# Context laid out as three chunks of 64 dims, projected in 64-row tiles, with a copy between keys and values

## The chip, the cores and the metric

The program runs on one core of one Trainium2 chip. A core has several engines that run side by side, each through its own instruction queue and strictly in that queue's order: TensorE (PE) for matmuls, VectorE (DVE), ScalarE (ACT), GpSimd (POOL), and SyncE (SP), which here only issues DMAs. Matmuls write to PSUM, which here is handed out in tiles; VectorE and ScalarE read results from there. The metric is the device time of one execution in microseconds, as the median of several runs.

## What is computed

A perceiver of four layers. `x` (128 tokens of 256) attends to a long context (12,544 tokens of 192), then to itself, then passes a feed-forward of experts. The part that matters here is the attention over the context in layers 0 to 2; layer 1 stands for the three (layer 0 has a mask in place of biases and clip, layer 2 no clip):

```python
def _L1_xattn_ref(query, key_value, Wq, bq, Wk, bk, Wv, bv, Wo, bo):
    H, D = 16, Cq // 16
    q = (query @ Wq + bq).reshape(B, Nq, H, D).transpose(0, 2, 1, 3)
    k = (key_value @ Wk + bk).reshape(B, Nkv, H, D).transpose(0, 2, 1, 3)
    v = (key_value @ Wv + bv).reshape(B, Nkv, H, D).transpose(0, 2, 1, 3)
    attn = jnp.clip(jnp.einsum('bhqd,bhkd->bhqk', q, k) * D ** -0.5, -CLAMP, CLAMP)
    attn = jax.nn.softmax(attn, axis=-1)
    attn = jnp.where(jnp.any(jnp.isnan(attn)), 1.0 / Nkv, attn)
    return jnp.einsum('bhqk,bhkd->bqhd', attn, v).reshape(B, Nq, Cq) @ Wo + bo
```

`key_value` is the context. It must be multiplied by Wk and Wv (192 x 256 each), which is the work that the change rearranges. Layer 3 does the same with 1,024 columns.

## The kernel before

All is in float32 but for a few small tiles. The context comes from memory with its dims on the partitions, in 25 blocks of 512 tokens (the last has 256). A block has two halves of 256 tokens. Its 192 dims do not fit 128 partitions, so it is held as two tiles: `ctxA` (dims 0 to 127, all 512 tokens, 256 KB) and `ctxB` (dims 128 to 191; half 0 on partitions 0 to 63, half 1 on 64 to 127; 128 KB). `Net.context` (L383) issues both loads, one block ahead of the one asked for, into four buffers each. Wk and Wv lie alike: the first 128 rows in one slab, the last 64 rows twice, once for each half of the partitions (`load_kv`).

`Keys` projects for layers 0 to 2. The 16 heads are taken in two groups `g` of 8, so `cols` picks 128 of the 256 columns. `project(g, b, low)` is called with `low` 0 and then 1. With `low` 0 it takes a PSUM tile `pair` (128 x 2 x 512, one 512-column part for each half of the block), and multiplies `ctxA` into keys (columns 0 to 255 of each part) and values (columns 256 to 511): two key products of 256 columns and four value products of 128 columns, over 128 rows. With `low` 1 it adds the `ctxB` products to the same places: two and four products over 64 rows, those of half 0 on the upper rows of the array and those of half 1 on the lower. Then ScalarE copies the keys out (`keep_keys`, L131, or L133 with bias) and after them the values (`keep_values`, L137). Every program matmul of float32 shows in the trace as two records.

`attend_twice` goes over the blocks twice for each group. In the first pass it finds the highest score of each query; its loop runs 25 steps. A step projects a block that later steps need (`keys.project`, both values of `low` in one go), and then makes score products in 32-row tiles:

- Layer 0 (`masked`): `highest` twice, each with two `pair` tiles of products (a mask row, L558, and the keys, L559), and VectorE reduces each pair to maxima (L565).
- Layers 1 and 2: `over` makes products with the difference of two blocks' keys (`apart`, made on POOL, L570) into two pairs, and ScalarE applies Relu to each (L578); then `highest_of_two` makes products with a block's keys into two more pairs, which VectorE adds and reduces (L586).

There are four `pair` tiles in the first pass (`psum(ppr=4)`), used in turn; a step that projects uses five. `in_order` fixes the order on TensorE, VectorE and ScalarE inside a step as the code has it. In group 0 of layers 1 and 2 the first 8 blocks are projected earlier, during the layer before, in a `kv` tile of which there is one (`early`, `early_pair`); in layer 0 the first two. Of the remaining blocks the last three are projected with keys only, their values by `project_values` near the end of the pass. The second pass makes weights and adds up values; at its end in group 0, blocks 0 and 1 of group 1 are projected.

In layer 1 POOL also adds up the whole context in group 0 (`add_up`), for a guard against NaN (`nan_guard`), which multiplies the sums by Wk and Wv.

Layer 3 uses `KeysInTurn`, a subclass of `Keys` with the same `keys_into` and `values_into` over `ctxA` and `ctxB`, two blocks at a time, with loads two blocks ahead.

The lines by which the profile names this work: L103 is every projection matmul (tiles `pair`, `kv` or `v`), L131 and L133 the key copies, L137 the value copies, L395 and L397 the loads of `ctxA` and `ctxB`.

Of the kernel before, what the change touches and what calls it, by code (L numbers as in the profile page):

```python
# [12 lines left out]
F32 = mybir.dt.float32  # L13
# [4 lines left out]
ALU = mybir.AluOpType  # L18
AX = mybir.AxisListType
PSUM = bass.MemoryType.PSUM  # L20

P = 128
D = 256
CD = 192
CB = CD - P
H = 16
S2 = 12544
SB = 512
HB = SB // 2
# [24 lines left out]
class Keys:  # L54
# [4 lines left out]
    def __init__(self, net, wk, wv, groups, bias=None, sums=None):  # L59
        self.net, self.nc, self.wk, self.wv, self.bias, self.sums = net, net.nc, wk, wv, bias, sums  # L60
        self.context = net.context(groups * NSB)
        self.started, self.done, self.rest = {}, 0, None
        if sums is not None:
            self.nc.gpsimd.memset(sums, 0.0)
# [30 lines left out]
    def add_up(self, g, b):  # L95
        if g == 0 and self.sums is not None:
            a, c = self.context(b)
            n = HB * len(self.halves(b))
            self.nc.gpsimd.tensor_tensor(self.sums[:, :n], self.sums[:, :n], a[:, :n], ALU.add)
            self.nc.gpsimd.tensor_tensor(self.sums[:, SB:], self.sums[:, SB:], c, ALU.add)  # L100

    def mm(self, out, a, b, low, start):
        self.nc.tensor.matmul(out, a, b, start=start and not low, stop=low == 1, skip_group_check=True)  # L103

    def keys_into(self, p, g, low, blocks, turn=None):

        cols = slice(g * P, g * P + P)
        for j, b in enumerate(blocks):  # L110
            ctx = self.context((g if turn is None else turn) * NSB + b)[low]
            for i, r in self.halves(b):
                r = r if low else slice(0, P)
                keys = ctx[r, :HB] if low else ctx[:, i * HB : (i + 1) * HB]
                self.mm(p[:, i, j * HB : (j + 1) * HB], self.wk[r, low, cols], keys, low, j == 0)

    def values_into(self, p, g, low, blocks, first=0, turn=None):
        cols = slice(g * P, g * P + P)
        for j, b in enumerate(blocks):
            ctx = self.context((g if turn is None else turn) * NSB + b)[low]  # L120
            for c in range(2):
                for i, r in self.halves(b):
                    at = first + (2 * j + c) * P
                    r = r if low else slice(0, P)
                    k = c * P if low else i * HB + c * P
                    self.mm(p[:, i, at : at + P], ctx[r, k : k + P], self.wv[r, low, cols], low, first + j + c == 0)
# [26 lines left out]
    def project(self, g, b, low, values=True):  # L153


        if g * NSB + b < self.done:
            return
        if not low:
            self.add_up(g, b)
            self.started[g, b] = self.net.early_pair() if self.rest is None else self.net.pair()  # L160
        p = self.started[g, b]
        self.keys_into(p, g, low, [b])
        if values:
            self.values_into(p, g, low, [b], HB)
        if low:
            n = len(self.halves(b))
            self.keep_keys(g, b, p[:, :n, :HB])
            if values:
                self.keep_values(g, b, p[:, :n, HB:])
            self.done = g * NSB + b + 1  # L170

    def project_values(self, g, blocks):
        p = self.net.pair()
        for low in range(2):
            self.values_into(p, g, low, blocks)
        for j, b in enumerate(blocks):
            self.keep_values(g, b, p[:, : len(self.halves(b)), j * HB : (j + 1) * HB])


class KeysInTurn(Keys):  # L180
# [5 lines left out]
    def __init__(self, net, wk, wv):  # L186
        self.net, self.nc, self.wk, self.wv = net, net.nc, wk, wv
        self.context = net.context((GROUPS3 + 1) * NSB, 2)
        self.first = {}

# [16 lines left out]
class Net:  # L207
# [123 lines left out]

    def load_column(self, src, pool, name):

        t = pool.tile([P, 2], F32, tag=name, name=name, bufs=1)
        self.nc.sync.dma_start(t, src.rearrange("o (g p) -> p (o g)", p=P))
        return t
# [46 lines left out]
    def context(self, until, ahead=1):  # L383

        nc, d = self.nc, self.d
        made = []

        def get(k):  # L390
            while len(made) <= k + ahead and len(made) < until:
                b = len(made) % NSB
                n = min(SB, S2 - b * SB)
                a = self.ahead.tile([P, SB], F32, tag="ctxA", name="ctxA", bufs=4)
                self.queue.dma_start(a[:, :n], d["ctxA"][:, b * SB : b * SB + n])  # L395
                c = self.ahead.tile([P, HB], F32, tag="ctxB", name="ctxB", bufs=4)
                self.queue.dma_start(c, d["ctxB"][b])  # L397
                made.append((a, c))
            return made[k]

        return get
# [617 lines left out]
    def l0_xattn(self, x):  # L1019
        nc, d = self.nc, self.d  # L1020
        with self.tc.tile_pool(name="x0", bufs=2, reuse_waits="tile") as pool:
            wk = self.load_kv(d["L0_xattn_Wk"], D, "wk", self.lw, nc.scalar)
            keys = Keys(self, wk, None, 2)
            keys.context(0)
            keys.wv = self.load_kv(d["L0_xattn_Wv"], D, "wv", self.lw, nc.scalar)
# [14 lines left out]
    def keys_biased(self, name, guarded):  # L1040

        nc, d = self.nc, self.d
        wk = self.load_kv(d[f"{name}_Wk"], D, "wk", self.lw)
        wv = self.load_kv(d[f"{name}_Wv"], D, "wv", self.lw)
        bk = self.load_column(d[f"{name}_bk"], self.lw, "bk")
        sums = self.lw.tile([P, SB + HB], F32, tag="sums", name="sums", bufs=1) if guarded else None
        keys = Keys(self, wk, wv, 2, bk, sums)

        self.queue = nc.gpsimd
        keys.early()  # L1050
        return keys
# [33 lines left out]
    def nan_guard(self, pool, totals, xT, wq, bq, wk, wv, bk, bv):  # L1085
# [4 lines left out]
        wide = pool.tile([P, 2, P], F32, tag="wide", name="wide")  # L1090
# [5 lines left out]
        def sums():  # L1096
            s = self.stat(2)
            nc.vector.tensor_reduce(s[:, 0:1], totals[:, :SB], AX.X, ALU.add)
            nc.vector.tensor_reduce(s[:, 1:2], totals[:, SB:], AX.X, ALU.add)
            nc.vector.tensor_copy(wide, bc(s, 2, P))  # L1100
            nc.gpsimd.memset(many, float(S2))

        def products(bank_pair):
            p = bank_pair()
            self.mm(p[:, 0, :D], [(xT[:, k, :], wq[:, k, :]) for k in range(2)] + [(self.ones[:1, :], bq)])
            self.mm(p[:, 1, :D], [(wide[:, k, :], wk[:, k, :]) for k in range(2)] + [(many, bk)])
            made.append(p)
            p = bank_pair()
            self.mm(p[:, 0, :D], [(wide[:, k, :], wv[:, k, :]) for k in range(2)])
            made.append(p)  # L1110
# [748 lines left out]
def layout(inputs):  # L1859
# [4 lines left out]
    ctx[:, :S2] = a["ctx_768"][0].T  # L1864
    given["ctxA"] = ctx[:P, :S2]
# [31 lines left out]
def program(given):  # L1897
    nc = bacc.Bacc("TRN2", target_bir_lowering=False, num_devices=1)
# [12 lines left out]
```

## Time and profile before

| | us |
|---|---|
| median of 3 runs | 3023.78 (3019.76 to 3024.86) |
| the profiled execution | 3021.48, of which the span of its instructions is 3019.8 |
| TensorE busy | 2882.8 (95%), mean granted clock 0.975 |
| VectorE, ScalarE, POOL busy | 2024.2, 1626.2, 282.7 |
| first pass with projections, layer 0 | 17.6 to 148 and 275.6 to 402, 5.62 a step in its regular part |
| first pass, layer 1 | 658 to 759 and 905.8 to 1027, 5.42 a step that projects |
| first pass, layer 2 | 1311 to 1413 and 1554 to 1674, 5.42 a step that projects |
| layer 3, keys and attention | from 1952 to about 2872, 9.35 for two blocks |

The stages are told by the starts of L103's key products on TensorE: a step is the time from one block's first key product to the next one's. "Busy" counts overlapping records once; records of matmuls overlap, since one starts before the one before it has ended. In a list of waits an engine is named with the line that waited, and after the arrow the engine and line whose work ended that wait.

### The profile page before, as it was taken

What the parts mean: (1) busy time and instruction counts of PE and PEld (TensorE: products, weight loads), DVE (VectorE), ACT (ScalarE), POOL (GpSimd) and SP (SyncE); (2) the same over time, 40 slices, a digit from 0 to 9 for tenths busy, and PEclk for the clock granted to TensorE, in tenths of its full rate; (3) what the DMA queues carried; (4) which work ended last, traced back from release to release, by engine and by line L of the source; (5) the groups of instructions that cost most, each with busy time, mean ns of one, the idle gap of its engine ahead of it and who ended that gap; (6) DMA issues with size and microseconds to landing.
All of it is one profiled execution on the core that took longest, in us unless ns stands there. A gap on an engine that the chain in (4) does not pass through costs nothing.

```text
span 3019.8 us, 79794 instructions
## 1 busy us (share of the span) xinstructions
PE 2882.8 (95%) x34893; PEld 2209.0 (73%) x34893; DVE 2024.2 (67%) x3241; ACT 1626.2 (54%) x1904; POOL 282.7 (9%) x504
## 2 busy tenths in 40 slices
PE   8999999989999999999999998899999999999969
PEld 5677667455676576765776675688989989889858
DVE  6876887525893598745544555577777777777844
ACT  1176148335685585245875682355655656555521
POOL 7011021223001100211001002000000000000000
PEclk9999999999999999999999998999999999999979
DMA  5201210562002202521012007232322223222436
GB/s 133 61 19 32 72 39 6 189 225 57 21 3 79 59 4 88 175 82 53 15 39 73 23 3 258 92 98 80 85 84 83 85 79 88 85 78 83 136 111 201
DMA packets 177706, 247.28 MB, mean 82 GB/s; under 512 B 32459, under 2 KB 119269, under 8 KB 177358
## 3 DMA queue, kind: packets, MB, share of 16 engines
q1 hardware_dynamic: 165592, 227.26, 24.8%
q0 software_dynamic: 11008, 14.37, 1.6%
q8 instruction: 274, 4.49, 0.6%
q10 hardware_dynamic: 758, 0.55, 0.1%
q14 instruction: 74, 0.61, 0.1%
HBM read 241.56 MB, written 0.13 MB: 80 GB/s over the span
## 4 chain that ended last, share of the span: by engine, by line
PE 83%; DVE 11%; ACT 2%; DMA 1%; issue 1%; SPq 1%; POOL 0%; ACTq 0%; DVEq 0%; POOLq 0%
PE pair L103 21%; PE acc L699 10%; PE pair L559 8%; PE v L103 8%; PE sc L859 6%; PE pair L629 5%; PE acc L901 5%; PE ps L279 5%; PE one L629 4%; DVE parts L565 3%; PE pair L622 2%; PE acc L279 2%; PE kv L103 2%; PE ps L1698 1%; DVE over L586 1%
## 5 line engine op out<-in xcount | busy, mean ns | idle before, releaser
L586 DVE CUSTOM_DVE_ANT_0 over<-over,pair 128x512 f32<-128x512 f32 x384 | 241.2, 683 | 249.2 <-PE pair L559 237.6
L103 PE MATMUL pair<-ctxA,wk 128*128 128x256 f32 x1236 | 328.7, 399 | 6.5 <-ACT over L578 1.8
L103 PEld LDWEIGHTS pair<-ctxA,wk 128*128 128x128 f32 x1236 | 217.0, 190 | 138.5 <-ACT over L578 53.0
L861 ACT COPY kept<-sc 128x1024 f32<-128x1024 f32 (+1 forms) x135 | 136.2, 1009 | 261.2 <-PE sc L859 261.2
L565 DVE TENSOR_REDUCE parts<-pair 128x2 f32<-128x1024 f32 (+1 forms) x216 | 235.7, 1157 | 41.8 <-PE pair L559 41.8
L290 DVE TENSOR_TENSOR top<-top,kept 128x1024 f32<-128x1024 f32 (+2 forms) x145 | 169.1, 1169 | 134.0 <-ACT kept L861 132.7
L293 DVE SCALAR_TENSOR_TENSOR e<-pair,floor 128x1024 f32<-128x1024 f32 x196 | 227.3, 1217 | 14.6 <-PE pair L629 14.6
L677 ACT ACTIVATE e<-pair 128x1024 f32<-128x1024 f32 x196 | 200.7, 1025 | 46.5 <-PE pair L629 26.0
L654 ACT ACTIVATE e<-e 128x1024 f32<-128x1024 f32 x196 | 206.7, 1057 | 35.3 <-DVE e L293 24.3
L629 PE MATMUL pair<-qz,kT 32*128 32x256 f32 x2112 | 218.9, 374 | 0.0
L699 PE MATMUL acc<-e,v 128*17 128x128 f32 x6336 | 211.4, 274 | 3.0 <-ACT e L692 2.2
L699 PEld LDWEIGHTS acc<-e,v 128*17 128x17 f32 x6336 | 155.8, 97 | 67.8 <-ACT e L692 45.6
L692 ACT ACTIVATE e<-e 128x1024 f32<-128x1024 f32 x196 | 205.0, 1048 | 0.0
L293 DVE SCALAR_TENSOR_TENSOR e<-one,maskcol,less 128x256 f32<-128x256 f32 x392 | 162.6, 477 | 53.3 <-PE one L629 43.3
L859 PE MATMUL sc<-qz,kT 64*128 64x128 f32 x2816 | 197.8, 279 | 0.0
L559 PE MATMUL pair<-kT,qz 32*128 32x512 f32 (+1 forms) x1120 | 192.7, 592 | 5.2 <-DVE parts L586 3.8
L578 ACT ACTIVATE over<-pair 128x1024 f32<-128x1024 f32 x192 | 186.9, 1021 | 14.7 <-PE pair L559 7.4
L103 PEld LDWEIGHTS v<-wv,ctxA 128*128 128x128 f32 x1568 | 189.8, 192 | 6.4 <-issue 1.7
L103 PE MATMUL v<-wv,ctxA 128*128 128x128 f32 x1568 | 193.1, 276 | 0.0
L103 PE MATMUL pair<-ctxB,wk 64*128 64x256 f32 x1236 | 188.9, 399 | 0.0
L290 DVE TENSOR_TENSOR e<-one,less 128x512 f32<-128x512 f32 x196 | 126.3, 686 | 88.6 <-PE pair L629 88.1
L859 PEld LDWEIGHTS sc<-qz,kT 64*128 64x128 f32 x2816 | 171.6, 187 | 13.0 <-issue 1.3
(457 smaller groups left out, 5637.7 us busy)
## 6 DMA issues: line engine op xcount, KB each, us to landing
ctxA<-in_ctxA SPq DMA_DIRECT2D x324, 256.0 KB
ctxB<-in_ctxB SPq DMA_DIRECT2D x339, 128.0 KB
w<-in_L_ffn_W SPq DMA_DIRECT2D x32, 1024.0 KB
ctxA<-in_ctxA POOLq DMA_DIRECT2D x36, 256.0 KB, 3.2
w<-in_L_ffn_w_gateT SPq DMA_DIRECT2D x8, 1024.0 KB
wu<-in_L_ffn_w_upT SPq DMA_DIRECT2D x8, 1024.0 KB
w<-in_L_ffn_w_downT SPq DMA_DIRECT2D x8, 1024.0 KB
w<-in_L_ffn_w1T SPq DMA_DIRECT2D x8, 1024.0 KB
```

Of the source, the lines that this page charges most:

```text
L103: self.nc.tensor.matmul(out, a, b, start=start and not low, stop=low == 1, skip_group_check=True)
L279: self.nc.tensor.matmul(out, lhsT, rhs, start=(i == 0), stop=(i == n - 1))
L290: self.nc.vector.tensor_tensor(out, a, b, op)
L293: self.nc.vector.scalar_tensor_tensor(out, a, s, b, op0, op1, **kw)
L559: nc.tensor.matmul(x, qz[r, g, s, :], k[r, :n], start=not by_mask, stop=True)
L565: nc.vector.tensor_reduce(parts[:, s, 2 * half : 2 * half + 2, i], x, AX.X, ALU.max)
L586: nc.vector.tensor_tensor_reduce(es[half][:, j, :], es[half][:, j, :], x[:, j, :], 1.0, -LARGEST, ALU.add, ALU.max, parts[:, s, 2 * half + ...
L629: nc.tensor.matmul(at, keys.kT(c // 4)[tiles[t], k], q, start=start, stop=True, skip_group_check=True)
L654: nc.scalar.activation(to, to, AF.Exp)
L692: nc.scalar.activation(to, to, AF.Exp)
L699: nc.tensor.matmul(acc[32 * t : 32 * t + 17, half, :], v[:, c % 4 + j, 4 * half + t, :], es[half][:, t // 2, j, t % 2, :], start=c + j + h ...
L859: nc.tensor.matmul(x[:, t, c : c + P], kT[r, c : c + P], qz[r, g, :], start=True, stop=True)
```

## The change

In layers 0 to 2 a block of context is one tile of 128 partitions x 3 x 256. Half 0 of the tokens lies on partitions 0 to 63, half 1 on 64 to 127; the middle index is the chunk of 64 dims. The host lays the input `ctx` out in this way, and one DMA of 384 KB loads it. Wk and Wv are held as three chunks of 64 rows, twice on the partitions (`load_twice`). Every projection product is over 64 rows: per block 6 for the keys and 12 for the values, in place of 4 and 8. `project` now has the keys in its first part, followed by their copy, and the values in its second, followed by theirs. `project_values`, `add_up` and the guard follow the new layout. Layer 3 keeps its layout and functions (moved into `KeysInTurn`); its A and B parts are now two regions of one tile, still loaded by two DMAs. The program also asks for a scratch of 8192 bytes for dynamic DMAs.

```diff
+CH = CD // CB
-        self.context = net.context(groups * NSB)
+        self.context = net.context(groups * NSB, whole=True)
...
-            a, c = self.context(b)
-            n = HB * len(self.halves(b))
-            self.nc.gpsimd.tensor_tensor(self.sums[:, :n], self.sums[:, :n], a[:, :n], ALU.add)
-            self.nc.gpsimd.tensor_tensor(self.sums[:, SB:], self.sums[:, SB:], c, ALU.add)
+            self.nc.gpsimd.tensor_tensor(self.sums, self.sums, self.context(b), ALU.add)
...
+    def keys_into(self, p, g, b):
         cols = slice(g * P, g * P + P)
+        ctx = self.context(g * NSB + b)
+        for c in range(CH):
             for i, r in self.halves(b):
+                self.mm(p[:, i, :HB], self.wk[r, c, cols], ctx[r, c, :], c == 0, c == CH - 1)
+
+    def values_into(self, p, g, b, first=0):
+        cols = slice(g * P, g * P + P)
+        ctx = self.context(g * NSB + b)
+        for half in range(2):
+            at = first + half * P
+            for c in range(CH):
+                for i, r in self.halves(b):
+                    self.mm(p[:, i, at : at + P], ctx[r, c, half * P : half * P + P], self.wv[r, c, cols], at + c == 0, c == CH - 1)
...
-    def project(self, g, b, low, values=True):
+    def project(self, g, b, part, values=True):
         if g * NSB + b < self.done:
             return
-        if not low:
+        n = len(self.halves(b))
+        if part == 0:
             self.add_up(g, b)
-            self.started[g, b] = self.net.early_pair() if self.rest is None else self.net.pair()
-        p = self.started[g, b]
-        self.keys_into(p, g, low, [b])
+            p = self.started[g, b] = self.net.early_pair() if self.rest is None else self.net.pair()
+            self.keys_into(p, g, b)
+            self.keep_keys(g, b, p[:, :n, :HB])
+            return
         if values:
-            self.values_into(p, g, low, [b], HB)
-        if low:
-            n = len(self.halves(b))
-            self.keep_keys(g, b, p[:, :n, :HB])
-            if values:
-                self.keep_values(g, b, p[:, :n, HB:])
-            self.done = g * NSB + b + 1
+            p = self.started[g, b]
+            self.values_into(p, g, b, HB)
+            self.keep_values(g, b, p[:, :n, HB:])
+        self.done = g * NSB + b + 1
...
+    def load_twice(self, src, n, name, pool, queue=None):
+        v = pool.tile([P, CH, n], F32, tag=name, name=name, bufs=1)
+        for i in range(2):
+            (queue or self.nc.sync).dma_start(v[i * CB : (i + 1) * CB], src.rearrange("(c p) n -> p c n", p=CB))
+        return v
...
-                n = min(SB, S2 - b * SB)
-                a = self.ahead.tile([P, SB], F32, tag="ctxA", name="ctxA", bufs=4)
-                self.queue.dma_start(a[:, :n], d["ctxA"][:, b * SB : b * SB + n])
-                c = self.ahead.tile([P, HB], F32, tag="ctxB", name="ctxB", bufs=4)
-                self.queue.dma_start(c, d["ctxB"][b])
-                made.append((a, c))
+                t = self.ahead.tile([P, SB + HB], F32, tag="ctx", name="ctx", bufs=4)
+                if whole:
+                    self.queue.dma_start(t, d["ctx"][b])
+                    made.append(t.rearrange("p (c k) -> p c k", c=CH))
+                    continue
+                n = min(SB, S2 - b * SB)
+                self.queue.dma_start(t[:, :n], d["ctxA"][:, b * SB : b * SB + n])
+                self.queue.dma_start(t[:, SB:], d["ctxB"][b])
+                made.append((t[:, :SB], t[:, SB:]))
...
-            self.mm(p[:, 1, :D], [(wide[:, k, :], wk[:, k, :]) for k in range(2)] + [(many, bk)])
+            self.mm(p[:, 1, :D], [(wide[:, k, :], wk[:, k, :]) for k in range(CH)] + [(many, bk)])
...
+    given["ctx"] = ctx.reshape(CH, CB, NSB, 2, HB).transpose(2, 3, 1, 0, 4).reshape(NSB, P, CH * HB)
...
-    nc = bacc.Bacc("TRN2", target_bir_lowering=False, num_devices=1)
+    nc = bacc.Bacc("TRN2", target_bir_lowering=False, num_devices=1, dynamic_dma_scratch_size=8192)
```

## The prediction

> **What bounds the kernel now.** I read the page's chain first:
>
> ```profile
> PE 83%; DVE 11%; ACT 2%; DMA 1%; issue 1%; SPq 1%; POOL 0%; ACTq 0%; DVEq 0%; POOLq 0%
> PE pair L103 21%; PE acc L699 10%; PE pair L559 8%; PE v L103 8%; PE sc L859 6%; PE pair L629 5%; PE acc L901 5%; PE ps L279 5%; PE one L629 4%; DVE parts L565 3%; PE pair L622 2%; PE acc L279 2%; PE kv L103 2%; PE ps L1698 1%; DVE over L586 1%
> ```
>
> TensorE carries 83% of it, and the projections of L103 are the largest item (layer 3's, which are also on L103, included). So the stage to read is the first pass of `attend_twice`, where each step projects one block. In layers 1 and 2 a step takes 5.42 us. TensorE's timeline of one step, then ScalarE's:
>
> ```profile
> 991.65 1.13 PE L103 MATMUL pair<-ctxA,wk 128*128 128x256 f32 x4
> 992.62 1.05 PE L103 MATMUL pair<-wv,ctxA 128*128 128x128 f32 x8
> 993.60 0.70 PE L103 MATMUL pair<-ctxB,wk 64*128 64x256 f32 x4
> 994.14 0.61 PE L103 MATMUL pair<-wv,ctxB 64*128 64x128 f32 x8
> 994.68 1.14 PE L559 MATMUL pair<-apart,qz 32*128 32x512 f32 x8
> 995.64 1.50 PE L559 MATMUL pair<-kT,qz 32*128 32x512 f32 x8
> ```
> ```profile
> 990.48 1.94 ACT L578 ACTIVATE over<-pair 128x1024 f32<-128x1024 f32 x2
> 994.80 0.69 ACT L133 ACTIVATE kT<-pair,bk 128x512 f32<-128x512 f32 x1 [2.38 <-PE pair L103]
> 995.38 0.58 ACT L137 COPY v<-pair 128x512 f32<-128x512 f32 x1
> 995.90 1.94 ACT L578 ACTIVATE over<-pair 128x1024 f32<-128x1024 f32 x2
> ```
>
> Columns: start, length, engine, line, what. Five `pair` tiles are needed per step and four exist, so a projection waits until the step before has freed its first one. The cycle closes through this:
>
> ```profile
> DVE over L586 <- PE pair L559: 46.4, 16, 2.9
> ...
> PEld pair L103 <- ACT over L578: 12.1, 16, 0.8
> ```
>
> These are the waits of 16 such steps (total, times, longest): the projection waits 0.76 us for the first L578. The ring is: projection 3.03 (991.65 to 994.68), difference products to the start of L578 1.22 (995.90), L578 1.02, its signal to TensorE 0.15; sum 5.42. VectorE idles 2.9 us a step, so it sets nothing.
>
> Layer 0 has another ring, of 5.62 us, through VectorE:
>
> ```profile
> 92.69 4.62 DVE L565 TENSOR_REDUCE parts<-pair 128x2 f32<-128x1024 f32 x4 [1.00 <-PE pair L559]
> ...
> 93.97 1.13 PE L103 MATMUL pair<-ctxA,wk 128*128 128x256 f32 x4
> ...
> 97.00 0.41 PE L558 MATMUL pair<-row,ones 32*128 32x512 bf16 x4
> ...
> 97.12 0.59 ACT L131 COPY kT<-pair 128x512 f32<-128x512 f32 x1 [4.54 <-PE pair L103]
> ```
>
> Projection 3.03, products to the first reduction 1.31 (97.00 to 98.31), reduction and signal 1.28. VectorE idles 1.00 us per step although it holds four reductions, so the projection's length is in this ring too. In both rings every us added to a projection is added to the step.
>
> **The change, part by part: one projection.** A program matmul shows as two records. Let p be the time of two paired 64-row records of 256 columns, v of 128 columns, l the first weight load that nothing hides, d the drain at a change of tile shape. From the starts above: L103's four B key records 2p+l=0.54, four A key records 4p+l=0.97, eight B value records 4v+d=0.54, eight A value records 8v+d=0.98. So p=0.215, l=0.11, v=0.11, d=0.10. The B rows show that two 64-row products in different row halves run side by side: eight records in the time of four.
>
> After: keys are three chunks for two halves, 6p+l=1.40; values 12v+d=1.42. Back to back that is 2.82 us against 3.03: the pairs cost what the old mixture cost, and one change of shape (128 to 64 rows) with its load is gone, −0.21. The Trainium skill, "TensorEngine Tiling (Array Packing)", section "Key Properties", says that changing the tiling mode drains TensorE. That agrees with d+l=0.21 here and would by itself give the −0.21.
>
> But the two parts are no longer back to back. In the changed program, as built, the first value product of a block waits for ScalarE's copy of that block's keys, in all 132 blocks with values (44 in each layer): the keys and the values of a half lie in one PSUM bank. Before, both copies followed all products. The wait lies in TensorE's queue: the value products stand behind it, then the step's score products, and ScalarE's L578 or VectorE's reduction behind these.
>
> Its price: the last key pair starts at l+5p=1.185, one such record lasts 0.376 (source view of L103), so keys end at 1.56. ScalarE starts 0.05 after the last record (994.75 to 994.80). The copy takes 0.69 with bias, 0.59 without. The signal back takes 0.15 (L578 ends 991.50, TensorE starts 991.65). ScalarE is free then: its second L578 ends 0.77 after the projection starts. Values start at 2.45 (layer 0: 2.35); they pay l again, so 12v+d+l=1.53, and the score products start at 3.98 (3.88) in place of 3.03. That is +0.95 (+0.85). In layers 1 and 2 L578 no longer queues behind the value copy (995.38 to 995.90 just covers its input's arrival), −0.05: +0.90.
>
> The skill's "PSUM — Partial Sum Buffer", section "Terms", has a rule that speaks against this change: two engines on one bank and quadrant at once are a collision error, so the copy and the value products of one bank must take turns. By that rule the price is +0.9 a step; without it, it would be −0.2. No run here shows such an error.
>
> Counts: layer 0 has 40 such steps in the loops; the first four last 7 to 11 us for loads, and I take half there: 36×0.85+4×0.43=32.3. Layers 1 and 2 have 14+20 each: 68×0.90=61.2.
>
> **The other parts.**
> - The end of the second pass in group 0, three times: two blocks are projected there. The first value wait also stands behind exponentials (until 905.29 in layer 1, projection from 902.73); other products of the order fill in for the second block. About 1.2 each by that timeline, bounds 0 and 2.6: +3.6.
> - The 18 blocks ahead of the loops: one `kv` tile, so a block now waits 1.2 us for the two copies of the one before; it will wait twice, about 0.9 and 0.6. Other layers' products stand between. +2, bounds −5 and 15 (18×0.85).
> - 18 keys-only blocks: 1.51 (0.97+0.54) becomes 1.40; layer 0's are covered by 4.62 us of reductions a step. 18 value-only projections lose about 0.2 each, not all on the path. Together −3.3.
> - The guard of layer 1: two more 128x256 products of about 0.44, +0.9; one reduction in place of two and one sum on POOL in place of two, hidden by the products of that stage.
> - Context loads: one 384 KB DMA for two in SP's and POOL's queues. SP requests them four blocks ahead, so nothing waits; 0. In layer 3 the A part now shares a buffer with B and is requested when B's products are done, 2402.61 in place of 2400.20, for use at 2415.08: over 12 us of cover; without it 2.4 us per pair of blocks.
> - Weights: each now twice on the partitions, 384 KB against 256 for the two; at the start keys wait for all of a block, while the first B keys started at 9.63 anyway. 0, ±1.
> - Half the scratch for POOL's descriptors: no row prices it. POOL's mask rows wait for TensorE, not the reverse (162.9 us in the second pass of layer 0). Taken as 0, the nearest bound; up to +5 if these rows came late.
>
> Sum: 32.3+61.2+3.6+2−3.3+0.9=96.7. On the profiled execution (3021.5 us, span 3019.8) 3118; on the median of the runs (3023.8, 2.3 above) 3120.
>
> **Rivals.**
> 1. The wait costs nothing, being over when TensorE comes to it, or not taking place: then 108 loop steps gain 0.21 to 0.26, about 25 us: 2999, faster. For it: the B rows and the drain. Against: keys end at 1.56, and a copy alone takes 0.59. It decides from a stall below 0.2 us a step.
> 2. The stall is partly covered: half of it taken up by slack in one of the rings: about 3024+50=3074. For it: TensorE idles 0.76 and 0.92 us a step. Against: those gaps end with the ring's own release, which moves along.
> 3. The stall is dearer: handshakes of 0.3 in place of 0.2 (108×0.1), early blocks and pass ends at their upper bounds (+13, +4), late mask rows (+5): 96.7+33=130, so 3154.
>
> **Numbers.** Forecast 80%, rival 1 5%, rival 2 8%, rival 3 7%. Prediction 3120. Range: 0.1 us on 108 steps is ±11, the bounds of early blocks, pass ends and scratch −9 to +22; together, combined as independent, about −18 and +25: 3102 to 3145, which leaves rivals 1, 2 and the far end of 3 out. A measurement of this kernel tells about 0.2% (6 us) from no change. Faster: rival 1 without its weakest end, 0.04; same 0.02 (its weakest end, and the lightest of rival 2); slower 0.94.
>
> **What will show it.** Steps of 6.3 us in layers 1 and 2 and 6.5 in layer 0; a TensorE wait of some 0.8 us for `kT`'s copy in each; value products starting 2.4 us after the key products; score products 3.9 to 4.0 after. Stages outside these loops unchanged, layer 3 at 9.35 us per pair. Wrong if value products follow the keys at once, if 64-row pairs take over 0.23 us, or if the steps lengthen by less than 0.5 us.

## The result, and the profile after

The changed kernel takes 3133.55 us (median of four runs, 3123.96 to 3137.24), beside 3023.55 us of the kernel before on the same chip (four runs, 3019.76 to 3024.86). The ratio is 1.0361, with a 95% interval of 1.0335 to 1.0387: slower by 110 us. The profiled execution took 3130.95 us, its span 3129.2 us, at a mean granted clock of 0.974 (before: 0.975).

The chain of work that ended last, from the page of the changed kernel, by engine and by line:

```profile
PE 80%; DVE 10%; ACT 6%; DMA 2%; issue 2%; POOL 1%; ACTq 0%; SPq 0%; DVEq 0%; POOLq 0%
PE pair L101 12%; PE acc L728 9%; PE v L184 8%; PE pair L184 7%; PE sc L888 6%; PE acc L930 6%; PE pair L658 5%; PE pair L588 5%; PE ps L297 4%; PE one L658 4%; DVE parts L594 3%; PE pair L651 2%; PE acc L297 2%; PE kv L101 2%; ACT over L607 2%
```

Before, ScalarE had 2% of this chain; now it has 6%. (L101 is the old L103 for layers 0 to 2; layer 3 now has its own line, L184. L607 is the old L578, L588 the old L559.) TensorE's busy time hardly moved, 2880.8 us where it was 2882.8, so the added time is not more TensorE work. The list of waits over 16 steps of layer 1, group 1 (total us, times, longest us), says what it is:

```profile
DVE over L615 <- PE pair L588: 62.4, 17, 3.7
...
PEld pair L101 <- ACT over L607: 18.1, 16, 1.1
PEld pair L101 <- ACT kT L127: 15.5, 13, 1.2
PE pair L101 <- ACT kT L127: 10.2, 13, 0.8
...
PE pair L101 <- ACT kv L127: 2.4, 3, 0.8
```

The waits on the key copy (L127) were not in this list before. It is there in each of the 16 steps, 13 times into a tile `kT` and 3 times into one named `kv`, and each time the matmuls stand 0.8 us (10.2/13, 2.4/3) for it. VectorE idles longer too, 3.7 us at most where it was 2.9.

One step of layer 1 on TensorE, then ScalarE in the same stretch (start, length, engine, line, what, and in brackets the idle time before it and what ended it):

```profile
1046.03 1.57 PE L101 MATMUL pair<-ctx,wk 64*128 64x256 f32 x12 [0.30 <-ACT over L607]
1048.39 1.61 PE L101 MATMUL pair<-wv,ctx 64*128 64x128 f32 x24 [0.79 <-ACT kT L127]
1049.92 1.14 PE L588 MATMUL pair<-apart,qz 32*128 32x512 f32 x8
...
1052.22 0.49 PE L101 MATMUL pair<-ctx,wk 64*128 64x256 f32 x2 [0.30 <-ACT over L607]
```
```profile
1047.65 0.69 ACT L127 ACTIVATE kT<-pair,bk 128x512 f32<-128x512 f32 x1 [0.75 <-PE pair L101]
1050.04 0.59 ACT L131 COPY v<-pair 128x512 f32<-128x512 f32 x1 [1.71 <-PE pair L101]
1051.15 1.94 ACT L607 ACTIVATE over<-pair 128x1024 f32<-128x1024 f32 x2 [0.52 <-PE pair L588]
```

Keys begin at 1046.03 and end at 1047.60; the copy runs from 1047.65 to 1048.34; the values begin 0.05 us after that. The step takes 6.19 us (1052.22 − 1046.03) in place of 5.42. In layer 0 the same picture, with the reductions of L594 closing the ring, gives 6.38 us (71.10 − 64.72) in place of 5.62:

```profile
64.72 1.57 PE L101 MATMUL pair<-ctx,wk 64*128 64x256 f32 x12 [0.24 <-DVE parts L594]
66.97 1.61 PE L101 MATMUL pair<-wv,ctx 64*128 64x128 f32 x24 [0.69 <-ACT kv L125]
...
71.10 0.49 PE L101 MATMUL pair<-ctx,wk 64*128 64x256 f32 x2 [0.24 <-DVE parts L594]
```

The added time by stage, from the starts of the score products in the two traces (after less before, us):

| stage | added |
|---|---|
| start of the span to the first score product (20.9 to 27.6) | +6.7 |
| six first passes (756.9 to 841.3) | +84.4 |
| six second passes | −0.4 |
| first pass to second pass, six times | −3.5 |
| ends of the second pass of group 0, three times | +5.8 |
| layer 0 to 1, layer 1 to 2 | +5.4, +10.0 |
| from the end of layer 2's second pass on, with layer 3 | +0.9 |
| sum | +109.3 |

The start can be read on its own. Layer 0's mask is requested behind the weights, 8.50 us into the span (6.46 before), and its cast on VectorE starts 4.88 us later than the 9.62 of before:

```profile
14.50 0.23 DVE L439 CAST mf<-m 98x128 f32<-98x128 uint8 x1 [2.82 <-DMA m<-in_mask]
```
```profile
15.37 0.32 PE L444 MATMUL tr<-ident,st 98*1 98x98 f32 x1 [3.00 <-DVE st L442]
15.62 2.93 PE L101 MATMUL kv<-wv,ctx 64*128 64x128 f32 x24
```

The first value products stand on TensorE behind a transpose that needs that mask. (Before, they stood ahead of it.)

### The profile page after: what moved, and what is told of

Its sections match the earlier page's. It is cut to its first block, busy times and chain, and to the rows that moved or that the text cites. A ratio compares the mean times of both kernels' runs of the same rounds, so it can differ in the third digit from the quotient of the medians.

```text
span 3129.2 us, 82688 instructions
## 1 busy us (share of the span) xinstructions
PE 2880.8 (92%) x36661; PEld 2186.3 (70%) x36661; DVE 2025.5 (65%) x3240; ACT 1642.4 (52%) x1904; POOL 270.5 (9%) x461
## 4 chain that ended last, share of the span: by engine, by line
PE 80%; DVE 10%; ACT 6%; DMA 2%; issue 2%; POOL 1%; ACTq 0%; SPq 0%; DVEq 0%; POOLq 0%
PE pair L101 12%; PE acc L728 9%; PE v L184 8%; PE pair L184 7%; PE sc L888 6%; PE acc L930 6%; PE pair L658 5%; PE pair L588 5%; PE ps L297 4%; PE one L658 4%; DVE parts L594 3%; PE pair L651 2%; PE acc L297 2%; PE kv L101 2%; ACT over L607 2%
## 5 line engine op out<-in xcount | busy, mean ns | idle before, releaser
L184 PEld LDWEIGHTS v<-wv,ctx 64*128 64x128 f32 (+1 forms) x3136 | 295.2, 190 | 12.0 <-issue 2.1
L184 PE MATMUL v<-wv,ctx 64*128 64x128 f32 (+1 forms) x3136 | 300.4, 274 | 0.0
L101 PE MATMUL pair<-wv,ctx 64*128 64x128 f32 x3096 | 213.2, 282 | 84.3 <-ACT kT L127 44.4
L594 DVE TENSOR_REDUCE parts<-pair 128x2 f32<-128x1024 f32 (+1 forms) x216 | 235.8, 1159 | 78.3 <-PE pair L588 78.2
L101 PEld LDWEIGHTS pair<-wv,ctx 64*128 64x128 f32 x3096 | 189.0, 190 | 136.8 <-ACT kT L127 67.2
L184 PE MATMUL pair<-ctx,wk 64*128 64x256 f32 (+1 forms) x1440 | 276.2, 384 | 1.2 <-ACT kT L212 1.1
L101 PEld LDWEIGHTS pair<-ctx,wk 64*128 64x128 f32 x1548 | 143.6, 189 | 140.6 <-ACT over L607 73.1
L101 PE MATMUL pair<-ctx,wk 64*128 64x256 f32 x1548 | 208.9, 397 | 27.3 <-ACT over L607 18.0
L184 PEld LDWEIGHTS pair<-ctx,wk 64*128 64x128 f32 (+1 forms) x1440 | 192.5, 189 | 34.2 <-issue 13.4
L607 ACT ACTIVATE over<-pair 128x1024 f32<-128x1024 f32 x192 | 187.0, 1021 | 53.2 <-PE pair L588 44.0
```

The lines of the kernel that those rows point to most:

```text
L101: self.nc.tensor.matmul(out, a, b, start=first, stop=last, skip_group_check=True)
L594: nc.vector.tensor_reduce(parts[:, s, 2 * half : 2 * half + 2, i], x, AX.X, ALU.max)
L607: nc.scalar.activation(e, x, AF.Relu)
```

## The experiments

Ten kernels ran, in four groups, each group beside the kernel before on its own chip.

**e1, the order undone, the layout kept.** In `project`, both copies come after the value products:

```diff
             self.keys_into(p, g, b)
-            self.keep_keys(g, b, p[:, :n, :HB])
             return
...
+        p = self.started[g, b]
         if values:
-            p = self.started[g, b]
             self.values_into(p, g, b, HB)
+        self.keep_keys(g, b, p[:, :n, :HB])
+        if values:
             self.keep_values(g, b, p[:, :n, HB:])
```

> The changed kernel, with one thing moved: the copy of the keys comes after the value products, as before the change, so that a block's 18 products run on end. Theory (the loss is TensorE's wait for the key copy, and 64-row pairs run as fast as the old mixture): a projection takes 2.82 us from its first key product to the score products, steps take about 5.41 us in layer 0 and 5.2 in layers 1 and 2, and the time is 3023.6 minus 108 x 0.21 plus up to 7 us of the slower start, 3000 to 3010. Rival (the layout itself is dear: three chunks, doubled weights, one large load): steps stay above 5.9 us and the time stays above 3090.

Measured: 3020.99 us, ratio 1.0003 (0.9988 to 1.0019). The steps are 5.42 us in layer 0 and 5.22 in layers 1 and 2, each 0.20 below before, as the theory had it; the time misses the 3000 to 3010 expected. TensorE, then ScalarE, in one step of e1:

```profile
975.75 1.57 PE L101 MATMUL pair<-ctx,wk 64*128 64x256 f32 x12
977.15 1.50 PE L101 MATMUL pair<-wv,ctx 64*128 64x128 f32 x24
978.58 1.14 PE L589 MATMUL pair<-apart,qz 32*128 32x512 f32 x8
...
980.97 1.35 PE L101 MATMUL pair<-ctx,wk 64*128 64x256 f32 x10
```
```profile
978.70 0.69 ACT L127 ACTIVATE kT<-pair,bk 128x512 f32<-128x512 f32 x1 [2.18 <-PE pair L101]
979.28 0.58 ACT L131 COPY v<-pair 128x512 f32<-128x512 f32 x1
979.80 1.94 ACT L608 ACTIVATE over<-pair 128x1024 f32<-128x1024 f32 x2
```

The projection takes 2.83 us (975.75 to 978.58), as the 2.82 of the prediction's sum for products back to back. So the early key copy carries the whole loss, and the layout alone nets nothing: 108 loop steps should have won 22 us, which did not arrive.

**e2, the order alone, the layout of before.** All key products of A and B, the key copy, then all value products:

```diff
-        self.keys_into(p, g, low, [b])
+        n = len(self.halves(b))
+        if not low:
+            for k in range(2):
+                self.keys_into(p, g, k, [b])
+            self.keep_keys(g, b, p[:, :n, :HB])
+            return
         if values:
-            self.values_into(p, g, low, [b], HB)
...
+            for k in range(2):
+                self.values_into(p, g, k, [b], HB)
+            self.keep_values(g, b, p[:, :n, HB:])
...
```

> The kernel before, with only the order changed: a block's A and B key products, the key copy, then its A and B value products. Theory (the wait belongs to the order, not to the layout): the first value product waits for the copy, and there are two more changes of tile shape per block, so steps lengthen by 0.75 to 1.1 us and the time is 3120 to 3160. Rival (the wait came with the 64-row layout): the time stays within 15 us of 3024.

Measured, in two runs: 3161.06 us, ratio 1.0462 (1.0440 to 1.0483), steps of 6.77 and 6.58 us: 1.15 and 1.16 longer than before, a little more than the 0.75 to 1.1 of the theory. TensorE in one step:

```profile
1050.77 1.13 PE L103 MATMUL pair<-ctxA,wk 128*128 128x256 f32 x4 [0.30 <-ACT over L580]
1051.83 0.70 PE L103 MATMUL pair<-ctxB,wk 64*128 64x256 f32 x4
1053.32 1.16 PE L103 MATMUL pair<-wv,ctxA 128*128 128x128 f32 x8 [0.79 <-ACT kT L133]
```

The same wait of 0.79 us, in the layout that had none: it belongs to the order. The loss is larger than in the changed kernel because this layout changes from A's shape to B's twice: from the first key product to the first value product it takes 2.55 us (2.36 there), from there to the score products 1.74 (1.53).

**e3 and e6, one tile and the scratch.** e3 is the kernel before with the A and B parts in one tile (as layer 3 has them after the change) and the 8192 bytes of scratch; e6 has the scratch only.

```diff
-                a = self.ahead.tile([P, SB], F32, tag="ctxA", name="ctxA", bufs=4)
...
-                c = self.ahead.tile([P, HB], F32, tag="ctxB", name="ctxB", bufs=4)
+                t = self.ahead.tile([P, SB + HB], F32, tag="ctx", name="ctx", bufs=4)
...
-    nc = bacc.Bacc("TRN2", target_bir_lowering=False, num_devices=1)
+    nc = bacc.Bacc("TRN2", target_bir_lowering=False, num_devices=1, dynamic_dma_scratch_size=8192)
```

> The kernel before, with only two side parts of the change: ctxA and ctxB as two regions of one tile (still two loads) in all four layers, and the scratch of 8192 bytes for dynamic DMAs. Theory: no change, 3018 to 3030, layer 3 at 9.35 us for two blocks. Rival (these parts carry some of the 13 us by which the forecast fell short): 3030 to 3045.

> The kernel before with only the scratch of 8192 bytes for dynamic DMAs asked for. The kernel before with this scratch and A and B parts in one tile took 0.31% longer (0.17 to 0.45). If the scratch did that, this run is 0.2 to 0.4% longer than before (3029 to 3034 where before is 3023.5); if the shared tile did (its load is requested only after the B products), this run agrees with before within 0.15%: 3019 to 3028.

Measured: e3 3032.93 us, ratio 1.0031 (1.0017 to 1.0045); e6 3020.56 us, ratio 0.9992 (0.9984 to 1.0001). The scratch costs nothing; the shared tile is what is left of e3, some 9 us, where the theory expected nothing (3032.93 lies in the rival's range). (The tile alone was not run.) Of this, 2.9 us stand in the list of waits: in group 0 of layer 1 TensorE waits four times for `apart`, the key difference that POOL makes (0.4 us before). The same wait is larger in e1, 4.3 us in all. TensorE, then POOL, in e1:

```profile
693.37 1.14 PE L589 MATMUL pair<-apart,qz 32*128 32x512 f32 x8 [1.18 <-POOL apart L600]
```
```profile
690.27 1.82 POOL L98 TENSOR_TENSOR sums<-sums,ctx 128x768 f32<-128x768 f32 x1 [3.03 <-DMA ctx<-in_ctx]
692.05 1.26 POOL L600 TENSOR_TENSOR apart<-kv 128x512 f32<-128x512 f32 x1
```

POOL's queue holds the sum over a later block ahead of the difference that is wanted now, and that sum waits for its block's load (landed at 690.27). The load is requested when a buffer comes free, which with one tile is after the last product of a block. Before, A's buffer came free earlier and POOL made the difference in time:

```profile
687.98 1.28 POOL L99 TENSOR_TENSOR sums<-sums,ctxA 128x512 f32<-128x512 f32 x1 [3.53 <-DMA ctxA<-in_ctxA]
689.21 0.73 POOL L100 TENSOR_TENSOR sums<-sums,ctxB 128x256 f32<-128x256 f32 x1
689.90 1.27 POOL L570 TENSOR_TENSOR apart<-kv 128x512 f32<-128x512 f32 x1
```

**e4, the value copy on VectorE.** e1 with the value copies of the loops of layers 1 and 2 moved from ScalarE to the idler VectorE:

```diff
-        self.nc.scalar.copy(to, p.rearrange("p i (h e) -> p i h e", e=16))
+        copy = self.nc.scalar.copy if self.bias is None or self.rest is None else self.nc.vector.tensor_copy
+        copy(to, p.rearrange("p i (h e) -> p i h e", e=16))
```

> As the first of these runs, and in layers 1 and 2 the value copies inside the loops are made by VectorE, which idles 2.9 us a step there. Theory: the pair tile of the projection comes free 0.6 us earlier, so the last pair of score products no longer waits, and the step falls from about 5.2 to 5.1 us (projection 2.82, score products to the first L607 1.22, L607 1.02, signal 0.05): 5 to 8 us faster than the first run. Rival (the copies were hidden behind the products): the same time as the first run within 2 us, or slower where VectorE's queue holds the copy up.

Measured: 3030.35 us, ratio 1.0035 (1.0020 to 1.0050); steps of 5.48 us in place of 5.22. The theory fell. ScalarE, then VectorE, then the weight load of the second pair of score products (here named `kv`) and the next projection:

```profile
961.34 0.69 ACT L127 ACTIVATE kT<-pair,bk 128x512 f32<-128x512 f32 x1 [2.43 <-PE pair L101]
```
```profile
962.06 0.69 DVE L132 COPY v<-pair 128x512 f32<-128x512 f32 x1 [1.76 <-ACT kT L127]
```
```profile
962.81 0.30 PEld L590 LDWEIGHTS pair<-kv,qz 32*128 32x128 f32 x4 [0.43 <-DVE v L132]
...
963.87 1.57 PE L101 MATMUL pair<-ctx,wk 64*128 64x256 f32 x12
```

The copies do not run side by side: VectorE starts 0.03 us after ScalarE has ended (961.34 + 0.69). So the value copy ends later, 4.36 us after the step's first key product (958.39 to 962.75; in e1 4.11, from 975.75 to 979.86). The last pair of score products starts 0.06 us behind it, and 1.06 us later comes the next projection: these 0.25 us are what the step has gained in length. In the program as built, two engines that only read one bank (here one tile, too) take turns, just as a write and a read do. That is the rule of the Trainium skill, "PSUM — Partial Sum Buffer", section "PSUM bank collisions raise a hardware error", which counts reads against reads; the trace agrees.

**e5, POOL's order.** e1 with POOL among the engines whose order is fixed in the first-pass loops of layers 1 and 2:

```diff
-                with self.in_order(*engines, before=chain):
+                with self.in_order(*engines, *([] if masked else [mybir.EngineType.Pool]), before=chain):
```

> The changed kernel with both copies behind the value products (as e1), and with GpSimd's instructions of the first-pass loops of layers 1 and 2 fixed in the order of the code too, so that the sum of a block's context stands in the queue at the step that projects this block, and not some three blocks ahead of the difference that TensorE needs next. Theory: in group 0 of layer 1 of e1, TensorE waits for the difference tile because a sum ahead of it on GpSimd waits for its block's load; with the order fixed that wait goes, the first pass of that group is 111 to 114 us in place of 119.5, other stages stay as in e1, and the total is 5 to 8 us below e1's 3021: 3012 to 3017, that is 0.2 to 0.3% faster than before. Rival (the wait has another cause, such as the load itself): that pass stays at 118 to 121 and the total at 3019 to 3023.

Measured: 3020.24 us, ratio 0.9991 (0.9979 to 1.0002). The wait for `apart` is gone, and three blocks of that loop take 19.05 us (20.3 in e1, 19.64 before). The pass takes 116.5 us, which misses the 111 to 114 expected: of what was gained, 3.3 us go to a wait of TensorE for VectorE at its end. The total misses the expected 3012 to 3017 too.

**e7, score products between keys and values.** The changed kernel, its early copy kept, with other products standing in the gap:

```diff
                     for step in steps[b]:
-                        keys.project(g, *step)
+                        if step[1] == 0:
+                            keys.project(g, *step)
...
                         es = over(g, i, s, less) if b < NSB - 1 else None
+                    for step in steps[b]:
+                        if step[1] == 1:
+                            keys.project(g, *step)
...
```

> The changed kernel with score products placed between a block's key products and its value products: in layer 0 one of the two sets, in layers 1 and 2 those with the difference of two blocks. So the key copy runs beside products that do not need it. Theory (the loss is TensorE idling for the copy, not work): most of the 0.8 us per step comes back; what stays is two more changes of tile shape (about 0.2 each with their weight loads), and in layers 1 and 2 the Relu that follows these products can delay nothing that the keys need, since their copy stands first in ScalarE's queue: steps of 5.5 to 5.9 us in layer 0 and 5.3 to 5.7 in layers 1 and 2 in place of 6.38 and 6.19, total 3045 to 3095. Rival A (the order of copies is the loss whatever stands between, since ring members only change places): steps stay above 6.0, total 3110 to 3135. Rival B (cover is complete): 3015 to 3030.

Measured: 3027.0 us, ratio 1.0016 (1.0002 to 1.0029): rival B. Steps of 5.45 and 5.24 us, within 0.03 of e1. TensorE in one step of layer 1:

```profile
994.18 1.57 PE L101 MATMUL pair<-ctx,wk 64*128 64x256 f32 x12
995.67 1.20 PE L588 MATMUL pair<-apart,qz 32*128 32x512 f32 x8
996.81 1.61 PE L101 MATMUL pair<-wv,ctx 64*128 64x128 f32 x24
998.35 1.14 PE L588 MATMUL pair<-kT,qz 32*128 32x512 f32 x8
999.42 1.57 PE L101 MATMUL pair<-ctx,wk 64*128 64x256 f32 x12
```

No line has a bracket: no group of matmuls begins with a wait. The copy still comes before the values, but 1.14 us of other products (995.67 to 996.81) now cover it. The two more changes of tile shape cost next to nothing on the whole: 5.24 us a step where e1 has 5.22. In e1 the `kT` products take 1.43 us (979.54 to 980.97), since their second pair waits for the value copy; here they take 1.07 (998.35 to 999.42), and the time goes to the changes of shape.

**e8 and e9, the rest of the cost.** e8 is e5 with layer 0's three mask loads requested right behind the key weights; e9 is e8 with five context buffers.

```diff
             wk = self.load_twice(d["L0_xattn_Wk"], D, "wk", self.lw, nc.scalar)
+            self.fetch_mask(pool)
...
-                t = self.ahead.tile([P, SB + HB], F32, tag="ctx", name="ctx", bufs=4)
+                t = self.ahead.tile([P, SB + HB], F32, tag="ctx", name="ctx", bufs=5)
```

> The kernel of e5 (changed layout, both copies behind the value products, GpSimd in order) with the three small loads of layer 0's mask requested right behind the key weights, and not behind all weights. In e5 the mask landed at 13.05 us where it landed at 9.62 before, and TensorE's first score product started at 24.3 in place of 20.9; after that TensorE was granted 0.95 of its clock from 17 to 148 us in place of 0.99, in one profiled execution each. If the late mask makes the late start, the first score product starts at 20.5 to 22; if the gap at the start is also what brings the half-clock stretch in that stage, its clock goes to 0.98 or more, which is worth about 5 us. Theory: both, total 3010 to 3015 where before is 3022 to 3023. Rival (the start waits for the weights' bytes, and the clock does not depend on it): start at 23 to 25, total as e5, 3018 to 3022.

> e8 with five buffers for context blocks in place of four, so that each block's load can be requested one block earlier. If the later request of the one-piece load still costs anything (the stages from layer 0 to 1 and the first pass in group 0 of layer 1, where the kernel before with A and B in one tile lost 5.3 and 3.7 us), those stages get 3 to 6 us shorter than in e8 and the total by as much. If GpSimd's order took all of that away, e9 agrees with e8 within 0.15%.

Measured: e8 3017.83 us, ratio 0.9995 (0.9983 to 1.0007); e9 3014.94 us, ratio 0.9983 (0.9968 to 0.9997). e8 lies between its two theories: the first score product starts at 22.8 us (24.3 in e5), not at 20.5 to 22, and the clock in layer 0's first pass is 0.97, not 0.98. In e9 the start is at 24.1 again with the mask requested in the same place, so a single profile does not fix it to better than a microsecond. Against e8, e9 is 0.12% faster, inside the 0.15% that was to be read as nothing left to gain: the first pass in group 0 of layer 1 takes 116.5 us in both, and the stage from layer 0 to 1, 134.8 in e9 and 139.6 in e8, is 135.5 in e5 with four buffers. e9 is the fastest of all kernels here; its interval ends just below 1, and 0.17% is less than a measurement of this kernel tells from no change.

**e10, the blocks ahead of the loops.** e1, with the early key copy only for the 18 blocks that are projected before the loops:

```diff
+            if self.rest is None:
+                self.keep_keys(g, b, p[:, :n, :HB])
             return
...
-        self.keep_keys(g, b, p[:, :n, :HB])
+        if self.rest is not None:
+            self.keep_keys(g, b, p[:, :n, :HB])
```

> The changed kernel with both copies behind the value products in the loops and at the ends of the second passes (as e1), but with the key copy ahead of the values for the 18 blocks that are projected ahead of the loops in the one kv tile. It takes apart what the order costs there. Against e1 (1.0003 of before): if these blocks wait for their copies but other layers' products fill in, as the prediction took it (+2), the ratio is 1.000 to 1.002, 3020 to 3028 us where before is 3022; if they pay the full 0.7 to 0.8 us each, as the stages between the layers in the profile of the changed kernel suggest (5.8 and 6.3 us longer than in e1), it is +12: 1.0035 to 1.005, 3033 to 3037 us.

Measured: 3028.4 us, ratio 1.0026 (1.0013 to 1.0038). Against e1 that is +0.0023 with an uncertainty of about 0.002, so 7 us, give or take 6: between the two theories. In the profile the stage from layer 0 to 1 is 6.1 us longer than in e1 (142.1 to 136.0), the stage from layer 1 to 2 is not (150.6 to 151.8). The first of these two stages takes 134.8 to 139.6 in e5, e8 and e9, which have e1's order there, so a single profile does not settle it.

## Why the prediction came out as it did

The forecast was slower, 3120 us in a range of 3102 to 3145; 3133.55 lies in it, 13.5 above the centre. Its mechanism is shown: the value products wait for the copy of their block's keys (the trace), the order alone brings that loss back in the old layout (e2), taking the order away removes it (e1), and so does covering it (e7). That the products wait because keys and values share a bank, and not only because they share a tile, no run shows: none put them into different banks.

Against the 96.7 of the prediction's sum the two traces show 109.3. The loops were put 9.1 too high, the stages between the layers 13.4 too low, the start 6.7 and the pass ends 2.2. That these errors partly cancel is luck; without the first the forecast would have been some 22 us short. Of the stages outside the loops, which were to stay as they were, layer 3 did (+0.9).

- **The wait itself.** Forecast +0.95 to the score products in layers 1 and 2, measured 3.89 − 3.03 = 0.86. The mis-sized member is the signal from ScalarE back to TensorE, put at 0.15 from the end of a Relu to the next projection; here it is 0.05. The start of the values came at 2.36 (forecast 2.45), in layer 0 at 2.25 (2.35).
- **The step.** Forecast 6.3 and 6.5, measured 6.19 and 6.38, that is +0.77 and +0.76 in place of +0.90 and +0.85. Besides the signal, the ring of layers 1 and 2 was misread in its last member. In the 5.42 us of before the Relu at 995.90 ended at about 996.92, and the last 0.15 us were taken for a signal. A second ring closed in that time: the second pair of `kT` products waited for the value copy (995.38 + 0.58), ran 1.06 us, and the next projection stood behind it. The same 0.05 and 1.06 us close the step of e1 (979.86 to 980.97), and in e4 the step grows with the end of the value copy. The two rings were nearly tied, so the sum was right though one member was not. In the changed kernel the Relu's ring alone closes: 3.89 + 1.23 (1049.92 to 1051.15) + 1.02 + 0.05 = 6.19.
- **The loops.** Forecast 93.5 over 108 steps; the six first passes grew by 84.4, which holds the smaller steps and also the late `apart` in group 0 of layer 1.
- **Pass ends.** Forecast 3.6 within 0 to 7.8; measured 5.8.
- **Blocks ahead of the loops.** Forecast +2 within −5 to 15. The stages between the layers grew by 15.4 together, but executions of one code differ there by several us (in the kernel before the stage from layer 1 to 2 was 148.1 us, in e6, which differs only by the scratch, 156.3). e10 puts the term at about 7, so it was sized too small, within its bounds.
- **Weights and start.** Forecast 0 ± 1; measured +6.7. The step that failed is "at the start keys wait for all of a block, while the first B keys started at 9.63 anyway". It followed the context and key weights only. Behind the larger requests came the mask, and behind the mask a transpose that stands in TensorE's queue ahead of the first block's values (a wait of 3.00 us). That place in the queue goes with the order of copies: in e1 the values stand ahead of the transpose, TensorE waits 0.62 us for it, and the first score product comes at 24.9; in e10, with the early copy in these blocks, the wait is 2.85 us and the product comes at 28.2. So 4.0 of the 6.7 us are left to the layout, and e8 and e9 do not tell how much of that is the mask.
- **Context loads.** Forecast "nothing waits; 0". In layer 3 that held: its stage grew by 0.9 us. In group 0 of layer 1 it did not: e1's first pass there is 7.4 us longer than before. The request moves from the last A product to the last product of the block, and the engine that suffers is POOL, whose sum stands ahead of a difference that TensorE needs.
- **Projections with keys or values alone.** Forecast −3.3; the stages from first to second pass, where the values are made, shrank by 3.5, and a step with keys alone in layers 1 and 2 went from 3.99 to 3.80 us. The guard's +0.9 was not measured by itself.
- **The scratch.** Forecast 0; e6 shows 0.

The second ring of before, in its step of the prediction's lines (the weight loads of the second pair and of the next projection):

```profile
996.01 0.30 PEld L559 LDWEIGHTS pair<-kT,qz 32*128 32x128 f32 x4 [0.17 <-ACT v L137]
...
997.07 0.19 PEld L103 LDWEIGHTS pair<-ctxA,wk 128*128 128x128 f32 x1 [0.76 <-ACT over L578]
```

Rival 1 (no wait) fell with the first trace. Rival 2 (half covered) has no support: the step took over all of the projection's 0.76 us in layer 0 and 0.77 of 0.86 in layers 1 and 2. Rival 3 had the right places, in the early blocks and pass ends, but dearer handshakes where they are cheaper; its 3154 is too high.

Why the better layout of e1 wins nothing can be followed by stage in its profiled execution (span 3014.8 us, before 3019.8). Four of its six first passes are shorter by 14.1 us together, which is the 0.2 us a step. Two places take most of it back. In group 0 of layer 1 the first pass grew by 7.4 us, of which 4.3 are the waits for `apart`. In group 0 of layer 0 it ends at 164.0 us in place of 160.8, where 20 shorter steps should have brought it forward by 4: the start is 4.0 late, and then VectorE's reductions stand behind waits of 8.1 and 5.8 us for the loads of two small weights, where before it waited 6.4 and 3.7 us for such loads. The 5 us that are left do not show in the medians (3020.99 and 3020.96), which goes with the clock, as the last section tells; what causes that was not found.

## What to carry to other kernels

When two results share a PSUM tile and bank, as here, a copy placed between their products is a wait in TensorE's queue; either keep both copies behind all products, or put independent products of at least the copy's length in the gap (here 1.14 us against a 0.69 us copy brought the step from 6.19 to 5.24). When separate loads become one, follow what stands behind the later request on every engine, the idlest too: a nearly empty GpSimd queue still delayed TensorE because its order put a patient instruction ahead of an urgent one. A saving per step is worth its count only if nothing in the other stages takes it back, so check the stages one by one.

## What the runs showed of the hardware

Kernels with the three-chunk layout and back-to-back products ran at a lower granted clock: 0.9715 in the mean of ten runs of e1 and 0.9704 in twelve of e5, beside 0.9747 in 87 runs of the kernel before (median 3022.0 us). Within one kernel the time follows the clock: in e1's runs a clock lower by 0.001 goes with 2.6 us more. Span times (1 − clock) is 86.1 us in e1 and 76.0 in its kernel before, so by this estimate some 10 us of the expected gain are lost there. (e1's profiled execution had 0.973 and took 3016.54 us.) In runs whose clock was 0.973 or 0.974 on both sides, before took 3024.3 us (33 runs), e1 3016.3 (4) and e9 3011.6 (3). In layer 0's first pass the profiled executions of before and of e5 differ in these rows by stretch (us, busy time and count of each engine, then the granted clock, the DMA share and GB/s):

```profile
17.00:148.00 131.00, 125.56 (x1029) 82.08 (x1027) 101.24 (x104) 24.44 (x46) 50.93 (x106) 0.99 0.33 86
```
```profile
17.00:148.00 131.00, 123.00 (x1295) 85.14 (x1294) 99.11 (x98) 24.07 (x46) 50.80 (x106) 0.95 0.36 92
```

But e6, the kernel before with the scratch, had 0.97 there, and so had e8, so the rows do not show that the layout's lower clock comes from this stage. The Trainium skill, "TensorE: Matmul & The Clock Gate", section "What's actually happening", says that a block that watches how busy TensorE has been sets its clock. The two rows fit that, with less busy time (123.00 us) at the lower clock, but over the whole span TensorE is busy 95% in before, e1 and e5 alike; no run here tells why this layout gets a lower clock.
